# Own PSUM bank pairs for the norm products of the column stages, another split of the last convolution chunk, and a shifted row of gate chunks

## The chip, the cores and the metric

One core of a Trainium2 chip runs the whole network in one launch. The metric is the device time of the launch in microseconds (us). Engines are named as in the profile: PE (TensorE), PEld (its weight loads), DVE (VectorE), ACT (ScalarE), POOL (GpSimd) and SP (SyncE, which here only issues DMAs). Each engine works through its own queue in program order.

## The reference

The input x is 4 images of 256 channels, 56 by 56, in fp32. Four layers follow one another, each of the form x + f(groupnorm(x)), with 32 groups of 8 channels:

```python
x = x + _L0_conv_ref(_gn(x), ...)   # involution: 7x7 taps per pixel, from two 1x1 products
x = x + _L1_conv_ref(_gn(x), ...)   # relu(x + bn(conv3x3(relu(bn(conv3x3(x))))))
x = x + _L2_conv_ref(_gn(x), ...)   # involution with batch norms and relu
x = x + _L3_conv_ref(_gn(x), ...)   # x * (channel gate) + x * (spatial gate from DFTs)
```

A group norm needs the mean and variance of each channel, then an average over the 8 channels of a group, then rstd and shift.

## The kernel before

The two 128-channel halves of an image are "blocks"; a pair (image b, half cb) is a **unit**, so there are 8 units, u = 2b + cb. The kernel runs `involution_layer(0)`, then `conv_layer`, then `involution_layer(2)`, into which layer 3 is folded as "gates".

**An involution unit** has two stages. In the **tap stage** (`tap_matrices`), 32 steps n each make two PE products (L613) into a PSUM pair of banks, which DVE (two steps of three, L634) or ACT (one of three, L627) empties into `kt`. In the **column stage**, seven columns tx are taken in turn by `apply`: PE multiplies `kt` with the windows `xw` (L659), first for five plus five rows of tiles in one pair of banks, then for nine in a second pair; ACT (L672 or L674) and DVE (L679, three times and once) empty them; POOL (layer 0, L684) or DVE (layer 2, L686) adds the result to the image. After each column come a transposition of the next strip (L427, seven products, in a pair of its own), its copy by ACT (L439) and four DMAs that shift the windows (L445, L446, on SP's queue), the next strip (L410 or L412), and `column_sums` (DVE, L1143).

**PSUM** is a pool of four pairs (`two_banks`). A pair goes back when everything that was ever read from it or written to it is done, and the next one to need a pair takes it.

**Small work is hung between the big steps by hand.** `hooks[n]` runs after tap step n; `late[tx]` runs after column tx. A list item is one step of a generator. The order in which Python emits instructions is each engine's order (`in_order`). `norm_steps` (L217) is such a generator, with nine steps: aggregate (DVE, L215); product with the group-average matrix (PE, L226); copy, subtract, square, add (DVE, L229 to L237); second product (PE, L240); rsqrt (DVE L150, POOL L151); shift (DVE, L244). `by_counts(g, (1, 1, 4, 1, 1, 1))` makes six steps of these nine. In the column stages the two products go to `spare[0]`, which `apply` sets (L652) to the second, unused bank of its second pair:

```python
for ng, tys, nty, rows in O_PARTS:
    pair = two_banks()
    spare[0] = pair[:, 1, :]
```

Norms run this way in every unit of layer 0 but the last and in unit 0 of layer 2. In the tap stages `spare[0]` is a corner of the tap pair; `gate_factors`, `first_half` and the layer-3 norms use that. The last step of the last image's `gate_factors` is taken after the column stage of unit 7, where it uses whatever `spare[0]` is then.

**The bottleneck** of the next image (`bottleneck`, L454) makes `hb` from one small product (L467; L476 in layer 0, L478 in layer 2), the products L489, and 20 ACT evacuations (L506, or L508 in layer 2) into `hp`, which the next taps read.

**The convolution layer** works in 12 chunks of rows (three an image). In a chunk's `conv2` the positions k run in the order 1, 2, 3, 4, 0, 5; `filtered_product` makes four groups of products for a k in two pairs (L1606) and combines them on DVE (L1618 to L1624); `middle` is L1633 and L1634. `after[...]` lists are hung between these as above. At a chunk's end `joined(co)`, for each half co, forms the result and adds x. For chunk 10, `added` does it: ACT relu (L1764), an accumulating DMA from POOL (L1765), a store from SP (L1766). For chunk 11, the last, both halves are done on DVE (L1752, then L1757, which is relu and addition in one), with a store (L1758). Channel sums of chunks 9 to 11 are taken by DVE `bn_stats` (`stats`, L1784): those of chunk 10 inside chunk 11's `conv2`, those of chunk 11 (`pending[0]`, six instructions) all at hook 3 of layer 2's first tap stage. Earlier chunks use ACT instead (`mean_of`, `spread_of`, L1768 to L1778).

**The gates**: layer 2's finished images wait in DRAM. `gate_chunk` brings in a piece of 8 rows (POOL DMA, L828), works four POOL instructions on it (L831 to L838) and stores it (POOL DMA, L841); `next_load` and `next_gate` take one step each. An image has 14 chunks: four in the column stage of the next image's first half, six in the tap stage and four in the column stage of its second half.

Of the kernel before, what the change touches and what calls it, by code (L numbers as in the profile page):

```python
# [16 lines left out]
P = 128  # L17
# [56 lines left out]
def net_kernel(  # L74
# [243 lines left out]
    def involution_layer(layer, xin, xout, red, span, sb, xs_of, ahead=None, pending=None):  # L318

        with ExitStack() as es:  # L320
# [130 lines left out]
            def bottleneck(b):  # L451
# [23 lines left out]
                if layer == 0:  # L475
                    nc.vector.tensor_add(hb, ps[:, 0:1], by_row(L0_RB))  # L476
                else:
                    nc.vector.scalar_tensor_tensor(hb, ps[:, 0:1], bn["s3"], bn["t3"], ALU.mult, ALU.add)  # L478
# [167 lines left out]
            def apply(b, cb, kt, tx, xw):  # L646
# [3 lines left out]
                for ng, tys, nty, rows in O_PARTS:  # L650
                    pair = two_banks()
                    spare[0] = pair[:, 1, :]  # L652
# [337 lines left out]

            hooks0 = {}
            if layer == 0:
                place(hooks0, begin(), (1, 2, 4, 6, 7))
            else:
                since = mark()
                nc.sync.dma_start(z_sb, z2_dram)
                nc.sync.dma_start(zb_sb, zb2_dram)
                next_strip()
                run(bottleneck(0))
                hooks0[3] = list(pending[0])  # L1000
                for _ in range(NXW - 1):
                    next_windows()
                    next_strip()
                hooks0[7] = [next_windows, next_strip]
            if layer == 0:
                next_strip()
                for i in range(NXW):
                    hooks0.setdefault(2 + 5 * i, []).extend((next_windows, next_strip))
# [34 lines left out]
            for u, (b, cb) in enumerate(units):  # L1043
                hooks = hooks0 if u == 0 else {}
                if prev is not None:
# [39 lines left out]
                if b + 1 < B:  # L1085
                    if layer == 0:
                        g = sums(b + 1, cb)
                        if cb == 0:
# [3 lines left out]
                            def norm_first():  # L1092
                                yield from norm_of(0, {u + 2: sums_of[b + 1, 0]}, u + 2, u + 3)

                            g = norm_first()
                            for tx in (3, 4, 4, 4, 4, 4, 5, 5, 6):
                                late[tx].append(step(g))
                        else:
# [3 lines left out]
                            def norm_last():  # L1102
                                yield from norm_of(0, {u + 2: sums_of[b + 1, 1]}, u + 2, u + 3)
# [3 lines left out]
                            late[2] += [step(g)] * 5  # L1107
# [11 lines left out]
                if layer == 2 and b > 0:  # L1119
                    if cb == 0:  # L1120
                        late[0] += [lambda b=b, j=j: load_sf(b - 1, j) for j in range(2)]
                    for tx in (1, 2, 4, 5) if cb == 0 else (0, 2, 3, 5):
                        late[tx] += [next_load, next_gate]
                if last_image and cb == 0:
                    g = norm_of(1, {}, 0, u)
                    for tx in (1, 2, 2, 2, 2, 2, 3, 3, 4):
                        late[tx].append(step(g))
                if layer == 2 and u == 0:
                    g = norm_of(2, dict(enumerate(pending[1], NB * (B - 1))), NB * (B - 1), NB * B)
                    for tx in (1, 2, 2, 2, 2, 2, 3, 3, 4):  # L1130
# [90 lines left out]
    def conv_layer(xin, xout, st, ahead):  # L1221
        with ExitStack() as es:
# [474 lines left out]
            def conv2(i, after, between, sums, tail):  # L1697
# [28 lines left out]
                def joined(co):  # L1726
# [29 lines left out]
                    if i == n_chunks - 1:  # L1756
                        stt(xj, rj, 0.0, xj, ALU.max, ALU.add)  # L1757
                        nc.sync.dma_start(xout[bb][co][:, at], x)  # L1758
# [3 lines left out]
                def added(x, xj, rj, co, at):  # L1762
# [3 lines left out]
                    nc.sync.dma_start(xout[bb][co][:, at], x)  # L1766
# [13 lines left out]
                def stats(co, k):  # L1780

                    r0, r1 = k * ST_ROWS, min(n, (k + 1) * ST_ROWS)
                    at = sum(ST_PIECES[: i % 3]) + k
                    nc.vector.bn_stats(sums[co][:, at, :], xr_of[i, co][:, r0 * W : r1 * W])  # L1784
# [45 lines left out]
                if not summed or bb == B - 1:  # L1830
# [60 lines left out]
            for s, (conv, i) in enumerate(order):  # L1891
# [47 lines left out]
                else:  # L1939
                    if i % 3 == 0:  # L1940
# [3 lines left out]
                            else small.tile([P, sum(ST_PIECES), 6], F32, name=f"st_c{co}", bufs=1)  # L1944
# [151 lines left out]
```

## Time and profile before

| what | value |
|---|---|
| median of 3 runs | 1666.82 us (1665.92 to 1667.41) |
| profiled execution, its own time | 1665.74 us |
| its span, first to last instruction | 1663.7 us |
| mean granted TensorE clock | 0.979 |
| POOL, busy | 552.1 us (33%) |
| PEld, busy | 1442.0 us (87%) |
| layer 0 (first instruction to the last L659 before the convolutions) | 0 to about 502 us |
| convolutions (to the last L1606) | about 502 to 1119.4 us |
| first tap stage of layer 2 begins (L613) | 1141.47 us |
| last L659 of layer 2 ends, final phase begins | about 1631.5 us |

Times are from the start of the span. In a row of the timeline come the start, the time until the group ends, the engine, the line of the kernel, the operation, what is written and read with its shape, the count, and in brackets the idle time just before it with what ended it. In a row of the waits come the engine, what it wanted to run, what released it, and the total, the number and the longest of these waits. In a row of the windows come the stretch, its length, the busy time (and count) of PE, PEld, DVE, ACT and POOL, the granted clock, the share of the DMA engines' time and GB/s.

### The profile page before, as it was taken

Reading aid. Unit: us, or ns where it says so; the run is one execution under the profiler, and the core shown is the slowest. Engines: PE = TensorE matmul, PEld = TensorE weight load, DVE = VectorE, ACT = ScalarE, POOL = GpSimd, SP = SyncE. Lnnn points to the kernel's source line nnn. Section 1 sums busy time; section 2 is a strip of 40 time slices with the busy share of each in tenths; the row PEclk is TensorE's granted clock in tenths of the full one; section 3 lists DMA queues with packets and bytes.
Section 4 is the critical chain, followed back from the end, with each engine's and each line's share of the span. In section 5 each row is a group of like instructions: output and inputs, shape, how many; then the busy total and the mean of one; then the engine's idle time right before and its main releaser. Section 6 shows DMA issues by size and latency. Waiting matters only on the chain.

```text
span 1663.7 us, 57362 instructions
## 1 busy us (share of the span) xinstructions
PE 1586.3 (95%) x24600; PEld 1442.0 (87%) x24600; DVE 1328.1 (80%) x2391; ACT 1010.6 (61%) x2203; POOL 552.1 (33%) x764
## 2 busy tenths in 40 slices
PE   6999999999989999999999999988999899899998
PEld 4997998898888898899999999976888888788886
DVE  2686887787659988899999999987777678678775
ACT  1655655557446565666666567426677577577565
POOL 2133223322522343423333333200000662662671
PEclk9999999999999999999999999998999999999997
DMA  2363445444558977987788797744445765764753
GB/s 92 111 197 115 157 155 169 146 156 132 181 171 266 171 130 150 198 174 157 159 166 170 163 197 151 172 144 145 131 140 166 216 220 188 210 216 159 206 168 113
DMA packets 102875, 275.67 MB, mean 166 GB/s; under 512 B 15877, under 2 KB 43790, under 8 KB 98910
## 3 DMA queue, kind: packets, MB, share of 16 engines
q0 software_dynamic: 43856, 106.25, 31.3%
q1 hardware_dynamic: 57726, 164.48, 30.7%
q8 instruction: 195, 3.19, 0.8%
q10 hardware_dynamic: 1040, 1.26, 0.3%
q14 instruction: 58, 0.48, 0.1%
HBM read 95.07 MB, written 49.15 MB: 87 GB/s over the span
## 4 chain that ended last, share of the span: by engine, by line
PE 68%; DVE 13%; DMA 6%; issue 6%; ACT 4%; SPq 1%; POOL 1%; ACTq 0%; POOLq 0%; DVEq 0%
PE ps L613 21%; PE mm L1606 17%; PE ps L659 15%; PE mm L1591 6%; DVE un L679 3%; PE ps L427 3%; DMA xw<-xw 2%; DVE kt L634 2%; PE ps L489 2%; DMA xs<-x 1%; ACT hp L508 1%; DMA xs<-v 1%; SPq L445 1%; DVE st L380 1%; ACT xs L1737 1%
## 5 line engine op out<-in xcount | busy, mean ns | idle before, releaser
L659 PE MATMUL ps<-kt,xw 126*32 126x48 f32 (+1 forms) x12544 | 378.9, 235 | 23.1 <-DMA xw<-xw 9.6
L659 PEld LDWEIGHTS ps<-kt,xw 126*32 126x32 f32 (+1 forms) x12544 | 340.9, 121 | 66.3 <-issue 40.4
L613 PE MATMUL ps<-hp,z_sb 64*126 64x133 f32 x6144 | 376.0, 278 | 1.8 <-ACT hp L508 0.9
L613 PEld LDWEIGHTS ps<-hp,z_sb 64*126 64x126 f32 x6144 | 364.1, 186 | 13.1 <-DVE kt L634 6.0
L634 DVE TENSOR_TENSOR kt<-ps,zb_sb 126x798 f32<-126x798 f32 x352 | 331.9, 980 | 48.9 <-PE ps L613 29.8
L627 ACT ACTIVATE kt<-ps,zb_sb 126x133 f32<-126x133 f32 x960 | 280.5, 441 | 78.1 <-PE ps L613 78.1
L1606 PE MATMUL mm<-xs,u_sb 128*128 128x140 f32 (+2 forms) x1664 | 210.3, 279 | 4.2 <-DMA xs<-v 4.1
L1606 PEld LDWEIGHTS mm<-xs,u_sb 128*128 128x128 f32 x1664 | 200.8, 192 | 4.6 <-issue 4.5
L1591 PE MATMUL mm<-v,u_sb 128*128 128x280 f32 (+2 forms) x864 | 193.9, 383 | 2.4 <-DVE hp L1622 1.7
L1591 PEld LDWEIGHTS mm<-v,u_sb 128*128 128x128 f32 x864 | 161.6, 189 | 28.0 <-PE mm L1606 2.2
L684 POOL TENSOR_TENSOR xs<-un,xs 128x240 f32<-128x240 f32 x112 | 72.0, 663 | 298.8 <-DVE un L679 298.7
L679 DVE SCALAR_TENSOR_TENSOR un<-ps,s,un 128x240 f32<-128x240 f32 x224 | 102.5, 458 | 85.2 <-ACT un L674 79.2
L679 DVE SCALAR_TENSOR_TENSOR un<-ps,par_sb,un 128x240 f32<-128x240 f32 x224 | 97.7, 456 | 84.3 <-ACT un L672 80.2
L1574 POOL DMA_DIRECT2D xs<-v x100 | 96.6, 1003 | 182.8 <-ACT xs L1573 161.7
L672 ACT ACTIVATE un<-ps,par_sb 128x240 f32<-128x240 f32 x112 | 50.2, 448 | 131.8 <-PE ps L659 121.0
L439 ACT COPY xw<-ps 126x896 f32<-126x896 f32 x112 | 101.3, 905 | 39.8 <-PE ps L427 22.0
L427 PE MATMUL ps<-ident_sb,strip_sb 128*126 128x128 f32 x784 | 112.7, 285 | 5.2 <-POOL strip_sb L412 2.0
L674 ACT ACTIVATE un<-ps,bn_t,s 128x240 f32<-128x240 f32 x112 | 60.1, 538 | 92.3 <-PE ps L659 85.2
L427 PEld LDWEIGHTS ps<-ident_sb,strip_sb 128*126 128x126 f32 x784 | 85.8, 142 | 16.1 <-POOL strip_sb L412 3.7
L1606 PE MATMUL mm<-v_sb,u_sb 128*128 128x140 f32 (+2 forms) x688 | 95.2, 281 | 3.2 <-ACT u_sb L1353 1.8
L1606 PEld LDWEIGHTS mm<-v_sb,u_sb 128*128 128x128 f32 x688 | 88.4, 193 | 4.3 <-ACT u_sb L1353 2.0
L1573 ACT ACTIVATE xs<-v 128x560 f32<-128x560 f32 (+2 forms) x100 | 61.8, 629 | 44.3 <-DVE v L1518 35.9
(325 smaller groups left out, 2344.2 us busy)
## 6 DMA issues: line engine op xcount, KB each, us to landing
xw<-xw SPq DMA_DIRECT2D x224, 252.0 KB
xw<-xw SPq DMA_DIRECT2D x224, 126.0 KB
xs<-x POOLq DMA_DIRECT2D x24, 560.0 KB, 6.9
x<-xs POOLq DMA_DIRECT2D x8, 1568.0 KB, 8.1
xs<-x SPq DMA_DIRECT2D x8, 1568.0 KB
xs<-v POOLq DMA_DIRECT2D x44, 280.0 KB, 4.3
xs<-v POOLq DMA_DIRECT2D x42, 252.0 KB, 4.2
xs<-in_x_dram SPq DMA_DIRECT2D x6, 1568.0 KB
```

The lines of the kernel that those rows point to most:

```text
L427: nc.tensor.transpose(ps[:Q, k * P : (k + 1) * P], flat[:, k * Q : (k + 1) * Q], ident_sb)
L439: nc.scalar.copy(xw[:, :NSB, :], ps[:Q, : NSB * P].rearrange("q (n c) -> q n c", n=NSB))
L613: nc.tensor.matmul(ps[:Q, i, k * NT : (k + 1) * NT], z_sb[i * R : (i + 1) * R, cb * GB // 2 + gp, z0 : z0 + Q], hp[i * R : (i + 1) * R, py ...
L627: nc.scalar.activation(kt[:, g0 + i, pb, :, k], ps[:Q, i, k * NT : (k + 1) * NT], AF.Identity, bias=zb_sb[:, cb * GB + g0 + i, p0 + k : p0 ...
L634: nc.vector.tensor_tensor(kt[:, g0 : g0 + 2, pb], ps[:Q, :, : PB * NT].rearrange("q i (k t) -> q i t k", k=PB), zb_sb[:, cb * GB + g0 : cb ...
L659: nc.tensor.matmul(v[m * j : m * j + m, i, :, k * TP : (k + 1) * TP], xw[:, window(ty), m * j : m * j + m], kt[:, ng * j : ng * j + ng, :, ...
L679: nc.vector.scalar_tensor_tensor(part, o[e], s, part, ALU.mult, ALU.add)
L684: nc.gpsimd.tensor_tensor(dst, u, dst, ALU.add)
L1573: nc.scalar.mul(t[:, at], v[:, below], -1.0)
L1574: nc.gpsimd.dma_start(t[:, at], v[:, at], accum_op=ALU.add)
L1591: nc.tensor.matmul(ps, *position(u, v, ci, dy, k, co, n), start=(j == 0), stop=(j == NB * 3 - 1))
L1606: nc.tensor.matmul(ps[:, bank, co * m : (co + 1) * m], u[ci][:, co * P : (co + 1) * P], v2[:, : n // 2, ci * WT : (ci + 1) * WT], start=(c ...
```

## The change

Five edits are in one diff.

1. The norms of the column stages get `norm_between`: the two products go each to a pair of their own (`one_bank`), in the six steps of `by_counts`, and the steps are spread anew over the columns. For image b + 1's first half in layer 0 the products stand after columns 4 and 6, the four DVE steps after column 5, and the shift moves to hook 5 of the next unit; for its second half both stand where they did; for the two norms of units 6 (layer 0) and 0 (layer 2) the six steps stand after columns 1 to 6. `apply` no longer sets `spare[0]`.
2. In layer 2, `hb` is made by ACT instead of DVE.
3. Chunk 11, half 0, ends like chunk 10 (ACT relu, accumulating DMA from POOL); half 1 stays on DVE. The two stores become entries of `pending[0]`.
4. Chunk 10's sums are taken by ACT (`mean_of`, `spread_of`, twice each), after the last `filtered_product`'s first part; the layout of the sums changes to triples. `pending[0]`, now two stores and six `bn_stats`, is spread over hooks 3, 5, ..., 17 of layer 2's first tap stage.
5. The gates of images 0 and 1 are spread three, six, four and one over four stages: three after columns 1, 3, 5, and one at hook 1 of the stage after next. Image 2 keeps four, six and four.

```diff
-                    nc.vector.scalar_tensor_tensor(hb, ps[:, 0:1], bn["s3"], bn["t3"], ALU.mult, ALU.add)
+                    nc.scalar.activation(hb, ps[:, 0:1], AF.Identity, bias=bn["t3"], scale=bn["s3"])
...
                     pair = two_banks()
-                    spare[0] = pair[:, 1, :]
...
+            def norm_between(layer, sts, u0, u1):
+                return by_counts(norm_steps(sts, one_bank, layer, u0, u1), (1, 1, 4, 1, 1, 1))
...
-                hooks0[3] = list(pending[0])
...
+                for n, f in enumerate(pending[0]):
+                    hooks0.setdefault(3 + 2 * n, []).append(f)
...
+                if layer == 2 and cb == 0 and b > 1:
+                    hooks[1].insert(0, next_gate)
...
+                if layer == 0 and cb == 1 and b + 1 < B:
+                    place(hooks, first, (5,))
...
-                            g = norm_first()
-                            for tx in (3, 4, 4, 4, 4, 4, 5, 5, 6):
+                            g = first = norm_first()
+                            for tx in (3, 4, 5, 6, 6):
                                 late[tx].append(step(g))
...
                             late[1].append(step(g))
-                            late[2] += [step(g)] * 5
+                            late[2] += [step(g)] * 2
                             late[3] += [step(g)] * 3
...
-                    for tx in (1, 2, 4, 5) if cb == 0 else (0, 2, 3, 5):
+                    for tx in (0, 2, 3, 5) if cb else (1, 2, 4, 5) if b == B - 1 else (1, 3, 5):
                         late[tx] += [next_load, next_gate]
...
-                    g = norm_of(1, {}, 0, u)
-                    for tx in (1, 2, 2, 2, 2, 2, 3, 3, 4):
+                    g = norm_between(1, {}, 0, u)
+                    for tx in range(1, 7):
...
-                    if i == n_chunks - 1:
+                    if i == n_chunks - 1 and co == 1:
                         stt(xj, rj, 0.0, xj, ALU.max, ALU.add)
-                        nc.sync.dma_start(xout[bb][co][:, at], x)
+                        tail.append([lambda: nc.sync.dma_start(xout[bb][co][:, at], x)])
                     else:
                         added(x, xj, rj, co, at)
...
-                    nc.sync.dma_start(xout[bb][co][:, at], x)
+                    store = lambda: nc.sync.dma_start(xout[bb][co][:, at], x)
+                    if i < n_chunks - 1:
+                        store()
+                    else:
+                        tail.append([store])
...
-                if not summed or bb == B - 1:
+                if i == n_chunks - 2:
+                    for f in (mean_of, spread_of):
+                        tail.append([lambda co=co, f=f: f(sums[co][:, 2 * ST_PIECES[0]], xr_of[i, co][:, : n * W]) for co in range(NB)])
+                elif bb == B - 1:
                     tail += [[lambda co=co, k=k: stats(co, k) for k in range(ST_PIECES[i % 3])] for co in range(NB)]
...
-                    loads_at = (2, 4) if i < n_chunks - 1 else (4, 7)
-                    for at, fs in zip(loads_at, tail2):
+                    for at, fs in zip((2, 4), tail2):
                         for k, f in enumerate(fs):
-                            after[at - (k == 0)].append(f)
+                            after[at - (k == 0) if i < n_chunks - 1 else 10].append(f)
```

More of the change, by code (lines that the diff above doesn't have):

```diff
@@ L1092, in norm_first @@
                             def norm_first():
-                                yield from norm_of(0, {u + 2: sums_of[b + 1, 0]}, u + 2, u + 3)
-                            g = norm_first()
-                            for tx in (3, 4, 4, 4, 4, 4, 5, 5, 6):
+                                yield from norm_between(0, {u + 2: sums_of[b + 1, 0]}, u + 2, u + 3)
+                            g = first = norm_first()
+                            for tx in (3, 4, 5, 6, 6):
                                 late[tx].append(step(g))
@@ L1102, in norm_last @@
                             def norm_last():
-                                yield from norm_of(0, {u + 2: sums_of[b + 1, 1]}, u + 2, u + 3)
+                                yield from norm_between(0, {u + 2: sums_of[b + 1, 1]}, u + 2, u + 3)
                             g = norm_last()
                             late[1].append(step(g))
-                            late[2] += [step(g)] * 5
+                            late[2] += [step(g)] * 2
                             late[3] += [step(g)] * 3
@@ L1121, in involution_layer @@
                         late[0] += [lambda b=b, j=j: load_sf(b - 1, j) for j in range(2)]
-                    for tx in (1, 2, 4, 5) if cb == 0 else (0, 2, 3, 5):
+                    for tx in (0, 2, 3, 5) if cb else (1, 2, 4, 5) if b == B - 1 else (1, 3, 5):
                         late[tx] += [next_load, next_gate]
                 if last_image and cb == 0:
-                    g = norm_of(1, {}, 0, u)
-                    for tx in (1, 2, 2, 2, 2, 2, 3, 3, 4):
+                    g = norm_between(1, {}, 0, u)
+                    for tx in range(1, 7):
                         late[tx].append(step(g))
                 if layer == 2 and u == 0:
-                    g = norm_of(2, dict(enumerate(pending[1], NB * (B - 1))), NB * (B - 1), NB * B)
-                    for tx in (1, 2, 2, 2, 2, 2, 3, 3, 4):
+                    g = norm_between(2, dict(enumerate(pending[1], NB * (B - 1))), NB * (B - 1), NB * B)
+                    for tx in range(1, 7):
                         late[tx].append(step(g))
@@ L1782, in stats @@
                     r0, r1 = k * ST_ROWS, min(n, (k + 1) * ST_ROWS)
-                    at = sum(ST_PIECES[: i % 3]) + k
-                    nc.vector.bn_stats(sums[co][:, at, :], xr_of[i, co][:, r0 * W : r1 * W])
+                    at = 2 * k + (2 * ST_PIECES[0] + 1) * (i == n_chunks - 1)
+                    st = sums[co][:, at : at + 2, :].rearrange("p a b -> p (a b)")
+                    nc.vector.bn_stats(st, xr_of[i, co][:, r0 * W : r1 * W])
                 for n_s, k in enumerate(KS[:5]):
@@ L1943, in conv_layer @@
                             if i // 3 < B - 1
-                            else small.tile([P, sum(ST_PIECES), 6], F32, name=f"st_c{co}", bufs=1)
+                            else small.tile([P, 2 * (ST_PIECES[0] + ST_PIECES[2]) + 1, 3], F32, name=f"st_c{co}", bufs=1)
                             for co in range(NB)
```

## The prediction

> **What bounds the kernel.** I read the busy shares of the page, then PE's waits, then the timeline at the places that the diff touches.
>
> ```profile
> PE 1586.3 (95%) x24600; PEld 1442.0 (87%) x24600; DVE 1328.1 (80%) x2391; ACT 1010.6 (61%) x2203; POOL 552.1 (33%) x764
> ```
>
> PE is busy nearly throughout, so a gain must come out of its idle time, place by place. The waits say where:
>
> ```profile
> ACT hp L508 <- DVE hb L478: 22.3, 1, 22.3
> ...
> PE ps L659 <- DMA xw<-xw: 9.6, 8, 3.6
> ...
> PE ps L467 <- DVE hp L1624: 5.2, 1, 5.2
> ...
> PE ps L226 <- DVE un L679: 4.9, 7, 1.0
> ...
> PE ps L240 <- DVE un L679: 4.4, 8, 1.0
> ...
> DVE st_c L1784 <- DMA u_sb<-x: 3.4, 1, 3.4
> ```
>
> Lines 4 and 5 are the norm products (9.3 us in 15 waits); lines 1, 3 and 6 belong to one place, the passage from the convolutions to layer 2; line 2 is where gate traffic could matter.
>
> **1. Norm products, -7.7 us.** A norm column of layer 0:
>
> ```profile
> 207.83 1.82 DVE L679 SCALAR_TENSOR_TENSOR un<-ps,par_sb,un 128x240 f32<-128x240 f32 x4 [0.72 <-ACT un L672]
> ...
> 208.22 0.98 PE L427 MATMUL ps<-ident_sb,strip_sb 128*126 128x128 f32 x7
> ...
> 209.56 0.62 DVE L1143 BATCH_NORM_STATS2 st<-xs 128x6 f32<-128x448 f32 x1
> ...
> 209.70 0.38 PE L226 MATMUL ps<-mv_sb,gavg_sb 128*128 128x1 f32 x2 [0.50 <-DVE un L679]
> ...
> 210.12 0.16 DVE L229 COPY gm<-ps 128x1 f32<-128x1 f32 x1
> ```
>
> PE is done with the transposition at 209.20, but the product writes a bank of the pair that DVE's fourth L679 still empties until 209.65, and waits 0.50. Its own input (L215) had been ready since 207.1. In a pair of its own it starts at once: all 9.3 us go. The Trainium skill (PSUM — Partial Sum Buffer, Summary: rules for kernel authors) says one may read PSUM while a matmul runs if the bank differs, and to guard by bank; by that rule alone the product could have run in its bank all along, part 1 would give nothing and the sum would be 1658. The row shows the program waiting nevertheless, so the row decides.
>
> What comes back: a fifth user of four pairs. The next `apply` then needs the pair of the `apply` just before, free when its third L679 is done. In layer 2 that is 1186.89 (row at 1185.41, 1.48 long), with the transposition over at 1186.76: 0.13 late, which the product itself (0.3) covers. Where the copy stands one column later, the pair is held for that column, and the following `apply` has no product to cover it: some 0.2 each. That is 7 times (three first halves, two products each in units 6 and 0): 1.4, and 0.2 for the rest. The nearest row is L467, a product already in its own pair at the same spot: the `apply` behind it started without a wait at 1235.20, but after 0.54 at 1359.66 and, in the same place one image on, 0.78. So the ends are -9.3 (nothing back) and +3.2 (0.78 after each of 16). I take -9.3 + 1.6, by the two rows of the columns themselves.
>
> **2. The passage into layer 2, -8.8 us.** DVE, then ACT and PE:
>
> ```profile
> 1109.92 0.63 DVE L1784 BATCH_NORM_STATS2 st_c<-u_sb 128x6 f32<-128x448 f32 x1 [3.43 <-DMA u_sb<-x]
> ...
> 1124.52 1.39 DVE L1752 SCALAR_TENSOR_TENSOR u_sb<-hp,s,u_sb 128x1120 f32<-128x1120 f32 x1
> 1125.94 2.20 DVE L1757 SCALAR_TENSOR_TENSOR xs<-u_sb,xs 128x1120 f32<-128x1120 f32 x1
> ...
> 1129.46 2.27 DVE L1757 SCALAR_TENSOR_TENSOR xs<-u_sb,xs 128x1120 f32<-128x1120 f32 x1
> ```
>
> ```profile
> 1133.29 8.34 ACT L508 ACTIVATE hp<-ps,hb,bn_s 64x168 f32<-64x168 f32 x20 [22.27 <-DVE hb L478]
> ```
>
> ```profile
> 1141.47 7.82 PE L613 MATMUL ps<-hp,z_sb 64*126 64x133 f32 x96 [0.85 <-ACT hp L508]
> ```
>
> The path is DVE to 1131.7, memsets, `hb` at 1133.07, ACT's 20 evacuations, taps. Six `bn_stats` of chunk 10 leave DVE (2.7 us), and with them the 3.43 wait for x. DVE takes L1618 at 1106.5, not 1110.46. Position 4 then waits for ACT's copy (L1617, over at 1108.7) and for PE (done 1110.2): 1110.95. L1810 to L1813 take 2.7 (1113.7), position 0 with `middle` 3.6 (1117.3), position 5 2.4 (1119.7). So L1752 stands at 1119.7, 4.8 earlier; L467 follows PSUM's release, so PE's 5.16 wait shrinks to under 2. One L1757 of two goes: L1752 twice (1122.5), L1757 once, DVE done at 1124.6, 7.1 earlier.
>
> ACT gets what DVE loses: `mean_of` 1.12 + 0.19 + 0.20 and `spread_of` 0.19 + 1.23 + 0.19 per half (rows L1771 to L1778), 6.2 in all, then a relu of 2.28 (row L1764). The means write x in place, so they wait for chunk 10's stores (L1766, issued from 1109.95). Those are over by 1116:
>
> ```profile
> 1116.00:1128.00 12.00, 6.84 (x39) 4.86 (x39) 11.65 (x17) 0.00 (x0) 0.00 (x0) 0.74 0.00 1
> ```
>
> (busy times of PE, PEld, DVE, ACT, POOL; then clock, DMA share, GB/s). ACT is idle in all of it, and no DMA runs. The first mean fits before 1116, the rest ends by 1120.7, before the relu can begin (1121.1). Relu to 1123.4, `hb` on ACT 0.2, and the evacuations start at 1123.7, not 1133.29: 9.6 earlier.
>
> Behind DVE and ACT stands all that allocates from the freed convolution memory: POOL's strip memset and strip (0.83 + 0.89, ready 1126.5, no later than PE), and SP's loads. SP loses two stores ahead of them (3.9 us of its time); `z_sb`, issued at 1133.5 before and used at 1141.47, is issued at 1126.4 and here by 1134.4 at the latest. POOL's accumulating DMA runs beside it. Taps so begin between 1131.9 and 1134.4; I take 1132.7, -8.8. PE's clock is the open end:
>
> ```profile
> 1140.00:1146.00 6.00, 5.15 (x47) 4.78 (x48) 2.49 (x4) 4.30 (x9) 0.00 (x0) 0.53 0.23 75
> ```
>
> The first 48 tap products ran at 0.53 and took 5.03 (chain of waits), against 2.9 at the 60 ns of the next 276: 2.1 to gain if that is spared. Products, two transpositions and then taps follow one another as thinly after the change, so I take 0. (The Trainium skill, TensorE: Matmul & The Clock Gate, HAM oscillation, wants no PE gap over some 3.4 us; by it the 5.16 gap, once under 2, would leave the clock up, 2.1 us better.) Ends: -11.7, and -4.8 (only DVE's own head start, ACT 4 us late).
>
> **3. Last `bn_stats`, -0.5.** All six stood at hook 3: 2.70 us on the chain at 1147.52, PE idle 0.40 and 0.48 around. Spread over 11 steps they need 2.7 of DVE's slack (two L634 of 0.91 in 2.05 us leave 0.9 in 12 steps, the transposition 1.0); the rest is eaten by the pairs ahead, or not. Ends -0.9 and +0.8.
>
> **4. Gates, -0.4.** POOL is not held by columns:
>
> ```profile
> 1326.75 0.54 POOL L841 DMA_DIRECT2D out_dram<-gx  x1
> 1335.97 0.56 POOL L151 TENSOR_TENSOR norm_sb<-norm_sb,mhalf 128x1 f32<-128x1 f32 x1 [8.68 <-DVE norm_sb L150]
> ```
>
> It takes six gates back to back from 1293.8 and is stopped only by the norm's power at step 12 of the next taps. With three instead of four in the column stage, five run before that stop, at the same pace: PE's 3.63 wait for `xw` at 1303.11 falls in the second gate and stays. Only the sixth (1321.8 to 1327) leaves the end of the stage, where waits of 0.4 stand. The fourteenth runs after 1382, beside taps. Ends -3.6 (that wait goes) and +0.6.
>
> **5. `hb` on ACT, three more times, 0**: 0.2 moves from DVE to ACT while PE works elsewhere; the waits behind L467 are for L679. Ends -0.6 and +0.6. **Unit 7, +0.9**: `spare[0]` is now the last tap pair, kept until the gate factors' product at the very end; the column stage has three pairs. Each `apply` behind a transposition (four) waits the 0.13 to 0.25 of part 1. Ends 0 and +4.7 (0.78 six times).
>
> **Sum.** -7.7 - 8.8 - 0.5 - 0.4 + 0 + 0.9 = -16.5. The profiled execution took 1665.74 (span 1663.7, 2.0 around it): 1649.2. The median of the runs is 1.1 higher: 1650.
>
> **Rivals.**
> - *The new pairs are the new wait.* If a held pair makes PE wait until DVE's copy, some 1.1 after the transposition (209.20 to 210.28), 7 times: 7.7 comes back in place of 1.6, 1656. For: DVE trails PE in every column. Against: another pair is free earlier.
> - *ACT or z_sb is late*, part 2 gives -4.8: 1654.
> - *The gates do relieve the windows*, -3.6: 1647. Against: POOL's pace.
> - *Slower: ACT's queue.* Four sums and a relu stand ahead of `hb` and the 20 evacuations. If the stores that the means wait for land late, each us moves the taps by one. Parts 1, 3, 4 and 5 give -7.7, so no change if the evacuations start at 1133.3 + 7.7 = 1141, and 0.2% slower from 1144.3: 1671 at 1145. It needs stores 20 us later than the 0.00 DMA share above allows.
> - *The diff does little*: 1666.
>
> **Chances.** Forecast (1646 to 1653) 0.57; pairs 0.15; ACT or z_sb 0.13; gates 0.09; slower 0.04; little 0.02. A measurement tells about 0.2% (3.3 us) from no change. Faster 0.94, within 0.2% 0.02, slower 0.04. The range reaches from the gates' case with the clock spared (1644) over the pairs' case (1658).
>
> **What would show it.** L226 and L240 without a wait on L679; under 0.3 before the `apply` behind. No L1784 between L1808 and L1618; L1752 near 1119.7 less what layer 0 saved; L508 starting some 9.6 earlier relative to the last L1606 of chunk 10; five gates before L151. Wrong if L659 waits on L229's copy, if L1771 ends after 1121, or if L613 waits for z_sb.

## The result and the profile after

| what | before | after |
|---|---|---|
| median | 1666.37 us (4 runs, 1664.09 to 1667.41) | 1645.28 us (4 runs, 1639.19 to 1647.76) |
| ratio, 95% interval | | 0.987, 0.9839 to 0.9901 |
| profiled execution, its own time | 1665.74 | 1639.19, the fastest of its four |
| span | 1663.7 | 1636.8 |
| mean granted clock | 0.979 | 0.985 |
| last L1606 (after: L1614) of chunk 11 to first tap product of layer 2 | 22.09 | 14.32 |

The changed kernel is 21 us faster; the forecast was 1650, in a range of 1644 to 1658. The median lies in the range and 0.7 us below the band of 1646 to 1653 that had the chance of 0.57. One of the six runs of the last experiment, 1666.73, was in a slow state and is left out of its ratio. Behind line 651 most line numbers moved: `apply`'s products are L658 (L659 before), its DVE step L678 (L679), the chunks' products L1599 and L1614 (L1591, L1606). The profiled execution is 6 us faster than its median, so what stands in one trace is read at the places of the change only, and a second profile of the changed kernel is used beside it (last experiment).

From the page of after, and from its waits (engine, line, released by: total, number, longest):

```profile
PE 1575.3 (96%) x24600; PEld 1435.7 (88%) x24600; DVE 1326.7 (81%) x2380; ACT 1020.6 (62%) x2220; POOL 555.5 (34%) x767
```

```profile
PE ps L658 <- DMA xw<-xw: 12.2, 15, 2.6
...
PE ps L658 <- DVE un L678: 5.8, 15, 1.2
...
PE ps L467 <- DVE hp L1632: 2.0, 1, 2.0
```

The waits of L226 and L240 for DVE's `un` and that of `st_c` are gone, and L467's is down from 5.2 to 2.0. L658's for DVE is up from 2.5 (5 times) to 5.8 (15 times): 1.2 of it stood there before, behind L489; 1.4 is three waits right behind L226, 1.4 is six waits a column later, and 1.7 is in unit 7. Those three parts came back, and with them some 0.13 at each of twelve places right behind the products (1.5 in all), too short for this row. The waits for windows are no smaller (9.6 before).

A norm column of layer 0 in the timeline of after, the one shown in the prediction:

```profile
204.09 1.82 DVE L678 SCALAR_TENSOR_TENSOR un<-ps,par_sb,un 128x240 f32<-128x240 f32 x4 [0.72 <-ACT un L671]
204.47 0.98 PE L427 MATMUL ps<-ident_sb,strip_sb 128*126 128x128 f32 x7
...
205.29 0.28 PE L226 MATMUL ps<-mv_sb,gavg_sb 128*128 128x1 f32 x2
...
205.71 3.27 PE L658 MATMUL ps<-kt,xw 126*64 126x96 f32 x112
...
208.91 0.98 PE L427 MATMUL ps<-ident_sb,strip_sb 128*126 128x128 f32 x7
...
210.11 3.26 PE L658 MATMUL ps<-kt,xw 126*64 126x96 f32 x112 [0.22 <-DVE un L678]
...
210.76 0.14 DVE L229 COPY gm<-ps 128x1 f32<-128x1 f32 x1
```

The product follows the transposition at once, while DVE still works (to 205.91) on the pair that it used to wait for, and the `apply` behind it starts 0.13 later. One column on, the product's pair is still held (its copy, L229, comes at 210.76), and the `apply` there waits 0.22 for L678. The passage into layer 2, same view:

```profile
1108.29 0.60 PE L467 MATMUL ps<-norm_sb,red_sb 128*128 128x1 f32 x4 [2.02 <-DVE hp L1632]
...
1108.93 0.35 ACT L478 ACTIVATE hb<-ps,bn_t,bn_s 128x1 f32<-128x1 f32 x1 [1.35 <-PE ps L467]
...
1109.69 2.26 ACT L1772 ACTIVATE xs<-u_sb 128x1120 f32<-128x1120 f32 x1 [0.40 <-DVE u_sb L1760]
...
1112.39 8.36 ACT L508 ACTIVATE hp<-ps,hb,bn_s 64x168 f32<-64x168 f32 x20 [0.43 <-PE ps L489]
...
1120.59 3.65 PE L613 MATMUL ps<-hp,z_sb 64*126 64x133 f32 x59 [0.91 <-DVE hp L497]
```

The last L1614 ended at 1106.27. ACT's evacuations start 6.1 behind it (13.9 before), the taps 14.3 behind it. What holds them in this trace is PE's own L489, whose first eight products took 3.42. In four other traces with the same passage (m_changed, e_spare, f_at3, k_gates0) the taps waited for z_sb, 1.1 to 2.0.

### The profile page after: what moved, and what is told of

Same layout as the page of the kernel before. It is cut to its first block, busy times and chain, and to the rows that moved or that the text cites. A ratio compares the mean times of both kernels' runs of the same rounds, so it can differ in the third digit from the quotient of the medians.

```text
span 1636.8 us, 57403 instructions
## 1 busy us (share of the span) xinstructions
PE 1575.3 (96%) x24600; PEld 1435.7 (88%) x24600; DVE 1326.7 (81%) x2380; ACT 1020.6 (62%) x2220; POOL 555.5 (34%) x767
## 4 chain that ended last, share of the span: by engine, by line
PE 73%; DVE 9%; DMA 6%; ACT 4%; issue 3%; SPq 2%; POOL 2%; ACTq 0%; POOLq 0%; DVEq 0%
PE ps L613 21%; PE mm L1614 20%; PE ps L658 14%; PE mm L1599 9%; DMA xw<-xw 4%; PE ps L427 3%; DVE un L678 2%; DVE kt L634 2%; PE ps L489 2%; SPq L445 1%; ACT hp L508 1%; SPq L446 1%; DMA xs<-v 1%; DMA xs<-x 1%; PE ps L971 1%
## 5 line engine op out<-in xcount | busy, mean ns | idle before, releaser
L658 PE MATMUL ps<-kt,xw 126*32 126x48 f32 (+1 forms) x12544 | 376.5, 234 | 25.6 <-DMA xw<-xw 12.2
L658 PEld LDWEIGHTS ps<-kt,xw 126*32 126x32 f32 (+1 forms) x12544 | 338.9, 121 | 70.1 <-issue 44.1
L613 PE MATMUL ps<-hp,z_sb 64*126 64x133 f32 x6144 | 374.1, 277 | 2.7 <-DVE hp L497 0.9
L613 PEld LDWEIGHTS ps<-hp,z_sb 64*126 64x126 f32 x6144 | 361.8, 185 | 13.5 <-DVE kt L634 6.1
L1614 PE MATMUL mm<-xs,u_sb 128*128 128x140 f32 (+2 forms) x1664 | 208.8, 278 | 1.8 <-DMA xs<-v 1.8
L1614 PEld LDWEIGHTS mm<-xs,u_sb 128*128 128x128 f32 x1664 | 199.7, 191 | 2.1 <-issue 1.7
L1599 PE MATMUL mm<-v,u_sb 128*128 128x280 f32 (+2 forms) x864 | 193.7, 382 | 1.5 <-DVE hp L1630 1.5
L1599 PEld LDWEIGHTS mm<-v,u_sb 128*128 128x128 f32 x864 | 161.8, 189 | 26.9 <-PE mm L1614 1.8
L678 DVE SCALAR_TENSOR_TENSOR un<-ps,s,un 128x240 f32<-128x240 f32 x224 | 102.5, 457 | 79.7 <-ACT un L673 75.5
L678 DVE SCALAR_TENSOR_TENSOR un<-ps,par_sb,un 128x240 f32<-128x240 f32 x224 | 97.9, 456 | 75.9 <-ACT un L671 71.9
L439 ACT COPY xw<-ps 126x896 f32<-126x896 f32 x112 | 101.4, 906 | 39.5 <-PE ps L427 21.9
L427 PEld LDWEIGHTS ps<-ident_sb,strip_sb 128*126 128x126 f32 x784 | 83.6, 140 | 14.7 <-POOL strip_sb L412 4.5
L1614 PE MATMUL mm<-v_sb,u_sb 128*128 128x140 f32 (+2 forms) x688 | 94.3, 279 | 2.1 <-ACT u_sb L1361 2.1
L1614 PEld LDWEIGHTS mm<-v_sb,u_sb 128*128 128x128 f32 x688 | 87.3, 191 | 3.0 <-ACT u_sb L1361 2.3
```

Source lines behind the costliest of these rows:

```text
L427: nc.tensor.transpose(ps[:Q, k * P : (k + 1) * P], flat[:, k * Q : (k + 1) * Q], ident_sb)
L439: nc.scalar.copy(xw[:, :NSB, :], ps[:Q, : NSB * P].rearrange("q (n c) -> q n c", n=NSB))
L613: nc.tensor.matmul(ps[:Q, i, k * NT : (k + 1) * NT], z_sb[i * R : (i + 1) * R, cb * GB // 2 + gp, z0 : z0 + Q], hp[i * R : (i + 1) * R, py ...
L658: nc.tensor.matmul(v[m * j : m * j + m, i, :, k * TP : (k + 1) * TP], xw[:, window(ty), m * j : m * j + m], kt[:, ng * j : ng * j + ng, :, ...
L678: nc.vector.scalar_tensor_tensor(part, o[e], s, part, ALU.mult, ALU.add)
L1599: nc.tensor.matmul(ps, *position(u, v, ci, dy, k, co, n), start=(j == 0), stop=(j == NB * 3 - 1))
```

## The experiments

Times are medians beside runs of the kernel before on the same chip, whose own medians were 1661.9 to 1666.4. "Passage" is the time from the last product of chunk 11 to the first tap product of layer 2; "to the norm" that from there to unit 0's first L226, less the wait before that L226; "window waits" are PE's idle times between two products of `apply` in a unit's column stage. These three are read from each kernel's one trace. Five traces (after, m_changed, e_spare, f_at3, k_gates0) have the changed kernel's passage and differ elsewhere: theirs is 14.17 to 15.11, so one trace tells a passage to about half a us. A ratio and its interval can differ by up to 0.2% from the quotient of the two medians beside them.

**1. The norm products alone (a_norms).** Edit 1 without the removed line of `apply`.

```diff
-                    g = norm_of(1, {}, 0, u)
+                    g = norm_between(1, {}, 0, u)
...
```

> The kernel before with edit 1 alone (pairs of their own for the norm products of the column stages; apply still sets spare[0], so unit 7 is as before). My theory, part 1: the 15 waits of L226 and L240 for L679 (9.3 us) go and 1.6 come back, so 7.7 less than before, about 1658.7 beside 1666.4; in its trace no product waits for L679, and the apply behind a product starts at most 0.5 late, only where the copy stands a column later. Rival (the new pairs are the new wait): PE waits about 1.1 at seven places until DVE's copy, so only 1.6 less. Rival (by the rule that only a shared bank has to be guarded): nothing changes, within 1 us of before.

Measured: 1656.87 beside 1665.55, ratio 0.9939 (0.9912 to 0.9966). No L226 or L240 waits for L679 (9.33 us in the trace of before). Right behind them stand 2.66 in all: 0.47 to 0.48 at three, 0.10 to 0.14 at ten. Six more waits of 0.24 to 0.28 (1.5 in all) stand at the `apply` one column later, where the pair is still held. So 5.2 is the gain at these places, half a us under the interval of the times (5.7 to 14.7 us). The theory holds but for the size of what comes back. Both rivals fall: 1.6 or nothing lie outside the interval.

**2. The passage alone (b_passage).** Edits 3 and 4, `hb` on DVE.

```diff
-                    if i == n_chunks - 1:
+                    if i == n_chunks - 1 and co == 1:
...
+                if i == n_chunks - 2:
+                    for f in (mean_of, spread_of):
...
```

> The kernel before with edits 3 and 4 alone (end of the convolutions; hb stays on DVE). My theory, parts 2 and 3: 8.8 and 0.5 less, no more, so 9.3 less than before, about 1657; PE's gap before L467 falls from 5.2 to 2. Second theory, from the trace of the whole change, where the first taps run at full clock and PE's 1.34 gap inside chunk 11 is gone: 1.3 and 2.1 more, so 12 to 13 less, about 1654. Rival (ACT or the tables late): 4.8 less, about 1661.6, with L613 waiting for z_sb or L508 for the second sum.

Measured: 1654.88, ratio 0.9939 (0.9915 to 0.9963), so 6 to 14 us less, which tells neither theory from the other. By the trace the passage is 16.59 (5.5 less) and the 1.34 inside chunk 11 is gone; PE's wait for L467 is 2.02. The rival is not seen: its 4.8 lies outside the interval, L613 waits for L508 and L508 for `hb`. The 1.34 comes and goes with x, though: in the four traces with chunk 10's sums on DVE, the wait of `st_c` for x is 1.9, 2.5, 3.1 and 3.4, and PE's wait inside chunk 11 is 0, 0.44, 1.0 and 1.34 (a_norms, h_sums10, c_gates, before). The clock was not spared: 0.61 over the first 4 us of taps. So the second theory's 2.1 did not come in this trace, and the passage is 2.3 longer than in the changed kernel, because ACT waited 2.73 for `hb`.

**3. The gates alone (c_gates).** Edit 5.

```diff
+                if layer == 2 and cb == 0 and b > 1:
+                    hooks[1].insert(0, next_gate)
...
-                    for tx in (1, 2, 4, 5) if cb == 0 else (0, 2, 3, 5):
+                    for tx in (0, 2, 3, 5) if cb else (1, 2, 4, 5) if b == B - 1 else (1, 3, 5):
```

> The kernel before with edit 5 alone (gate chunks three, six, four and one). My theory, part 4: POOL runs the gates at its own pace, so the 3.63 wait for xw in unit 2 stays: 0.4 less, which can't be told from no change. Rival (the gates relieve the windows): 3.6 less, about 1662.8, with that wait gone or halved.

Measured: 1666.95, ratio 1.0005 (0.9981 to 1.003). Window waits of units 2 and 4: 4.8 and 2.5 (before 4.2 and 5.7). POOL stored five gates ahead of L151 instead of six, as the prediction had it. The rival's 3.6 is outside the interval, by little.

**4. `spare[0]` back in `apply` (e_spare).**

```diff
                     pair = two_banks()
+                    spare[0] = pair[:, 1, :]
```

> The changed kernel with one line back: apply sets spare[0] to the unused bank of its second pair, so that unit 7's column stage has four pairs again. My theory (unit 7): 0.9 less than the changed kernel, so 22 less than before where the changed kernel is 21 less. Rival (three pairs are a wait in every column): up to 4.7 less than the changed kernel. Rival (they cost nothing): the same as the changed kernel.

Measured: 1650.2, ratio 0.9897 (0.9864 to 0.993), too wide for 0.9. By the traces: in unit 7 the changed kernel waits 0.28 and 0.26 for L678 behind two transpositions (in both of its profiles; 0.26 to 0.27 behind a third in three other traces), this one nowhere. It also waits 1.18 at the second column, which follows the first without a transposition between. After, then this kernel:

```profile
1579.99 3.23 PE L658 MATMUL ps<-kt,xw 126*64 126x96 f32 x112 [1.18 <-DVE un L678]
```

```profile
1584.59 6.90 PE L659 MATMUL ps<-kt,xw 126*64 126x96 f32 x224
```

The 1.18 stands in all seven traces with three pairs in unit 7 and in none of the seven with four. So three pairs cost 1.7 to 2.0 in waits there, not 0.9, and no wait in every column. The stage's length does not tell it (29.6 to 32.2 with four pairs, 30.0 to 33.5 with three), for its waits for windows vary by more.

**5. `hb` back on DVE (d_hb_dve).**

```diff
-                    nc.scalar.activation(hb, ps[:, 0:1], AF.Identity, bias=bn["t3"], scale=bn["s3"])
+                    nc.vector.scalar_tensor_tensor(hb, ps[:, 0:1], bn["s3"], bn["t3"], ALU.mult, ALU.add)
```

> The changed kernel with edit 2 undone (hb of layer 2 on DVE again). My prediction put edit 2 at nothing in the units and counted hb on ACT inside the passage. Theory now, from edits 3 and 4 alone, where hb stood on DVE behind the second L1758 and the strip's memset and L508 began 8.4 after the last convolution product (6.1 in the changed kernel): L508 begins about 2.3 later than in the changed kernel, taps about 2 later, units alike, so some 2 slower than the changed kernel. Rival (ACT's relu or the tables hold the passage anyway): the passage is as long as in the changed kernel, 14.3.

Measured: 1651.31, ratio 0.9898 (0.9867 to 0.9929). The passage is 17.32, 3.0 longer than in after (2.2 to 3.2 against the five traces); the rival is out. Timeline:

```profile
1118.67 0.20 DVE L404 MEMSET strip_sb<- 128x168 f32 x1 [1.81 <-POOL strip_sb L391]
1118.78 0.10 DVE L478 SCALAR_TENSOR_TENSOR hb<-ps,bn_s,bn_t 128x1 f32<-128x1 f32 x1
...
1118.99 8.34 ACT L508 ACTIVATE hp<-ps,hb,bn_s 64x168 f32<-64x168 f32 x20 [2.47 <-DVE hb L478]
```

On DVE the one-column `hb` stands behind L1765 and a memset that waits for POOL; ACT waits 2.47 for it.

**6. Half 0 back on DVE (g_half0).**

```diff
-                    if i == n_chunks - 1 and co == 1:
+                    if i == n_chunks - 1:
```

> The changed kernel with edit 3 undone (both halves of chunk 11 end on DVE; no relu on ACT, no accumulating DMA at the end). My theory, part 2: one L1752 and L1757 stand between the last convolution and the freed memory, one L1757 (2.3) more than in the changed kernel, so everything that allocates from it (strip, z_sb) is 2.3 later; L508 itself, with hb on ACT and no relu ahead, starts no later. Taps 1 to 2.3 later. Rival (the accumulating DMA and z_sb collide, so that edit 3 costs what it saves): taps no later than in the changed kernel, z_sb landing in less time from its issue.

Measured: 1644.68, ratio 0.9873 (0.9824 to 0.9922). Passage 15.21, 0.9 longer than in after, and 0.1 to 1.0 against the five traces. z_sb is issued 2.2 later, as the theory said, but the taps do not wait for it. They wait for ACT, which starts late for a reason that neither theory had:

```profile
1110.19 1.39 DVE L1760 SCALAR_TENSOR_TENSOR u_sb<-hp,s,u_sb 128x1120 f32<-128x1120 f32 x1
...
1111.70 8.36 ACT L508 ACTIVATE hp<-ps,hb,bn_s 64x168 f32<-64x168 f32 x20 [3.72 <-DVE u_sb L1760]
```

L508 writes `hp`, and the wait ends with the second L1760, the last reader of the convolutions' `hp`. With edit 3 both L1760 stand back to back; without it an L1765 of 2.2 stands between them. L489's first eight products, which ACT needs too, began at 1107.52 and at after's 3.42 were done by some 1110.9, so the extra wait is only the last 0.7. The rival (a collision that eats the gain) is not shown: the taps don't wait for z_sb. Edit 3 is worth up to 1.0, not 2.3, and the times don't tell it.

**7. Chunk 10's sums back on DVE (h_sums10).**

```diff
-                if i == n_chunks - 2:
-                    for f in (mean_of, spread_of):
-                        tail.append([lambda co=co, f=f: f(sums[co][:, 2 * ST_PIECES[0]], xr_of[i, co][:, : n * W]) for co in range(NB)])
-                elif bb == B - 1:
+                if bb == B - 1:
...
+                    loads_at = (2, 4) if i < n_chunks - 1 else (4, 7)
...
```

> The changed kernel with chunk 10's sums back on DVE (six bn_stats inside chunk 11's second convolution). My theory, part 2: DVE loses 4.8 there (the wait for x, then 2.7 of work), PE waits about 1.3 inside chunk 11 and about 5 instead of 2 before L467, so the taps come 4 to 5 later: 4 to 5 slower than the changed kernel. Rival (the sums were hidden; the gain came from edit 3 and hb alone): at most 1 later.

Measured: 1651.75, ratio 0.9929 (0.9901 to 0.9956): 12 less than before, where the changed kernel was 21 and, in its second set, 19 less. Passage 18.20, 3.9 longer than in after (3.1 to 4.0 against the five); inside chunk 11 PE waits 0.44. From its waits:

```profile
PE ps L467 <- DVE hp L1632: 5.2, 1, 5.2
...
DVE st_c L1797 <- DMA u_sb<-x: 2.5, 1, 2.5
```

Both waits of before are back. So of the passage's 7.8, by leaving out one at a time, chunk 10's sums are 3.9, `hb` 3.0 and half 0 0.9, each to about half a us.

**8. All of `pending[0]` at hook 3 (f_at3).**

```diff
-                for n, f in enumerate(pending[0]):
-                    hooks0.setdefault(3 + 2 * n, []).append(f)
+                hooks0[3] = list(pending[0])
```

> The changed kernel with all of pending[0] (two stores, six bn_stats) at hook 3 of layer 2's first tap stage. My theory, part 3: PE idles twice, 0.4 and 0.5, around the run of six, and waits nowhere else for them: the first taps' stage 0.5 to 0.9 longer than in the changed kernel. Rival: spread or not, DVE has the slack, and the stage is within 0.2.

Measured: one run, 1652.3. Around the six (2.78 on DVE) PE waits 0.42 and 0.47, as before; the changed kernel has one wait of 0.64 in its taps instead, for ACT's `kt` (so have all the kernels with the hooks spread). Spreading is worth 0.25: between the two theories.

**9. No gate in the first column stage (k_gates0).** Images 0 and 1: none, seven, four and three.

```diff
-                    hooks[1].insert(0, next_gate)
+                    for n, f in ((1, next_load), (1, next_gate), (3, next_load), (3, next_gate), (5, next_gate)):
+                        hooks.setdefault(n, []).append(f)
...
-                        for n in (2, 6, 14, 18, 22, 26):
+                        for n in (2, 6, 14, 18, 22, 26) if b == B - 1 else (2, 6, 10, 14, 18, 22, 26):
...
-                    for tx in (0, 2, 3, 5) if cb else (1, 2, 4, 5) if b == B - 1 else (1, 3, 5):
+                    for tx in (0, 2, 3, 5) if cb else (1, 2, 4, 5) if b == B - 1 else ():
```

> The changed kernel with the gates of images 0 and 1 spread none, seven, four and three (hooks 1, 3 and 5 of the stage after next) over the four stages, instead of three, six, four and one; image 2 as it was. In the eight kernels so far the column stages of units 2 and 4 hold 5 to 11 us of PE's waits for windows xw, those of units 1 and 3 at most 3, whether three or four gates are issued there. Theory (part 4: POOL runs five gates there in either kernel, and their transfers hold up the windows): with none issued, the waits of units 2 and 4 fall from some 8 together to under 2, and none appear in the tap stages: 6 to 7 less than the changed kernel, 27 less than before. Rival (the windows are late of themselves): units 2 and 4 keep 5 or more, no gain. Rival (the waits move): units 3 and 5 gain what 2 and 4 lose.

Measured: 1647.19 beside 1661.91, ratio 0.9916 (0.9894 to 0.9939): not better than the changed kernel by its ratio. Window waits of units 2 and 4: 2.0 and 2.0, between the theory's under 2 together and the rival's 5. They did not go; POOL still stored three gates there (five in the changed kernel), but that these hold up the windows is not shown. Units 3 and 5 hold 1.1 and 0.0, so nothing moved.

**10. Three small edits (j_mends).**

```diff
-                return by_counts(norm_steps(sts, one_bank, layer, u0, u1), (1, 1, 4, 1, 1, 1))
+                return by_counts(norm_steps(sts, one_bank, layer, u0, u1), (1, 2, 3, 1, 1, 1))
...
                     pair = two_banks()
+                    spare[0] = pair[:, 1, :]
...
             if layer == 2:
+                nc.sync.dma_start(z_sb, z2_dram)
+                nc.sync.dma_start(zb_sb, zb2_dram)
                 sin_sb = wpool.tile([H, H], F32, name="sin_sb")
...
```

> The changed kernel with three small edits at three places: norm_between in steps of 1, 2, 3, 1, 1, 1, so that the copy of the first product stands in the product's own column; spare[0] set in apply again; z_sb and zb_sb ahead of the two tables in SP's queue. Theory (the held pair costs the three waits of 0.48 behind L226; unit 7's transpositions are followed by 0.25 only with three pairs; z_sb is what L613 waits for where the clock stays up through L489): the 0.48 become 0.1 to 0.15, unit 7's 0.28 and 0.26 go, and L613 does not wait for z_sb: 1.5 to 2.4 less than the changed kernel, at the edge of what the times can tell. Rival on the copy (DVE now waits for PE's product with its column's work queued behind): the 0.48 stay or appear one apply later.

Measured: 1650.04, ratio 0.9934 (0.9908 to 0.9959): no gain over the changed kernel by the times. The three 0.48 stay (0.47, 0.47, 0.48). My theory of them falls, and so does the rival's reason: in those units the copy stood in the product's column already. Timeline of after at one of them:

```profile
136.53 0.34 DVE L215 BATCH_NORM_AGGREGATE mv_sb<-st 128x2 f32<-128x42 f32 x1
...
136.79 1.75 DVE L678 SCALAR_TENSOR_TENSOR un<-ps,par_sb,un 128x240 f32<-128x240 f32 x4
...
137.59 0.28 PE L226 MATMUL ps<-mv_sb,gavg_sb 128*128 128x1 f32 x2
...
138.34 3.27 PE L658 MATMUL ps<-kt,xw 126*64 126x96 f32 x112 [0.48 <-DVE un L678]
```

The wait is for L678, the release of the `apply` before, and L678 begins late because L215 and three sums of the next image (L380, 1.66) stand ahead of it on DVE. Where the pair really is held for a column, the `apply` right behind the product waits at most 0.14; the price comes one column later, 0.22 to 0.27 at six places in after (1.40 in all). Here the copy of the first product stands in the product's own column, and four of the six are gone. Timeline of j_mends at the place shown for after:

```profile
209.72 0.14 DVE L229 COPY gm<-ps 128x1 f32<-128x1 f32 x1
...
213.17 3.31 PE L659 MATMUL ps<-kt,xw 126*64 126x96 f32 x112
```

The two that stay (0.22 and 0.26) belong to the second products of unit 6 and of layer 2's unit 0, whose pair this edit still holds for a column. Unit 7's waits for L678 are gone. z_sb is issued 7.16 behind the last convolution product (7.99 in after), and L613 waits for DVE's copy; the passage is 14.39.

**11. Both (l_all).** Experiments 9 and 10 in one kernel.

```diff
+                    for n, f in ((1, next_load), (1, next_gate), (3, next_load), (3, next_gate), (5, next_gate)):
...
+                return by_counts(norm_steps(sts, one_bank, layer, u0, u1), (1, 2, 3, 1, 1, 1))
...
```

> Both at once: the gates none, seven, four and three, and the three small edits. Theory: the sum, 8 to 9 less than the changed kernel, some 29 less than before. Rival (windows late of themselves): only the small edits, 2 less than the changed kernel.

Measured: 1640.44 (1635.57 to 1641.88), ratio 0.9879 (0.9856 to 0.9902); passage 13.94, window waits of units 2 and 4 2.7 and 2.8. All five runs are below the six of j_mends on the same chip (1644.2 to 1655.97), which has the gates of the change. That points to the gates as a gain here; but k_gates0 against the changed kernel shows none, and the twelve other traces hold 5.2 to 10.5 in these two units, this one 5.5. Whether it beats the changed kernel stays open.

**12. The changed kernel again (m_changed).** No edit.

> The changed kernel once more, for more runs and a second profile of it. Edits 1, 3 and 4, and 5 alone measured -0.61%, -0.61% and +0.05%, together 1.17% or 19.5 us; edit 2 is worth 2 to 3 us inside the passage by its traces. Theory (the parts add up): 1.1 to 1.4% less than before, the passage 14 to 15 long, the waits for windows of units 2 and 4 5 or more together, and slower by 5 to 9 us than the kernel with the gates spread none, seven, four and three and the three small edits, where the chip is the same. Rival (the first four runs of the changed kernel were lucky): under 1% less.

Measured: 1648.74 (6 runs, 1640.31 to 1666.73) beside 1664.85, ratio 0.9884 (0.9846 to 0.9922). The parts add up within the intervals: 0.61, 0.61 and -0.05% make 1.17%, the whole 1.3 and 1.2%. The rival's "under 1%" lies inside this interval too, so these runs do not rule it out. The chip was another than that of l_all, so the two are not compared. Its profiled execution, 1656.84, has the same places: 2.8 right behind the norm products and 1.2 a column later, passage 14.82. Timeline:

```profile
1115.58 2.24 ACT L1772 ACTIVATE xs<-u_sb 128x1120 f32<-128x1120 f32 x1
...
1117.91 8.35 ACT L508 ACTIVATE hp<-ps,hb,bn_s 64x168 f32<-64x168 f32 x20
...
1126.77 5.80 PE L613 MATMUL ps<-hp,z_sb 64*126 64x133 f32 x96 [1.42 <-DMA z_sb<-z_dram]
```

Here x came late (ACT's first sum waited 3.99 for it), the four sums ended 3.5 behind the last convolution product (1.3 in after), and L508 started right behind the relu, no later than in the first profile (6.0 behind the last product). The taps then waited for z_sb.

## Why the prediction was right, step by step

| step | predicted | measured at its place |
|---|---|---|
| 1, norm products | -9.3 + 1.6 | -9.3 + 4.3 (after), + 4.0 (second profile) |
| 2, passage | -8.8 | -7.8 and -7.3, with the 1.34 inside chunk 11 of before: -9.1 and -8.6 |
| 2, clock at the taps | 0, with 2.1 open | to the norm 39.80 before, 37.56 after; 2.0 without the `bn_stats`' share |
| 3, `bn_stats` | -0.5 | -0.25 |
| 4, gates | -0.4 | no change that can be told |
| 5, `hb` in the units | 0 | not told apart |
| unit 7 | +0.9 | +1.7 |
| sum | -16.5 | -5.0 - 9.1 - 2.0 - 0.25 + 1.7 = -14.6 |

The measured terms make 1651.8 of the median before. They are a little short of the first ratio's interval (16.5 to 26.8 us less) and inside that of the second set (13.0 to 25.6). The trace of after is 26.9 shorter; most of what goes beyond 15 lies where the diff changes nothing: the start of the kernel (first taps at 43.62 instead of 45.69) and the convolutions ahead of chunk 11 (5.5 shorter; L1606's waits for transfers fall from 4.1 to 1.8). So the mechanisms were right. That the sums lie so near is luck in part: the terms that were off have both signs, and the clock's 2.0 did not come in every trace of this passage.

*Step 1.* The product's wait went as said. The held pair came back as said too: 0.2 at seven places, 1.4 in all, was forecast; after has 0.22 to 0.27 at six, 1.40 in all, and experiments 10 and 11 take away the four of them that they should. What the prediction missed is the place right behind the product, where it had 0.2 in all and after has 2.9: some 0.13 at twelve places, which the product was to cover and did not, and three waits of 0.48, over the 0.3 that the prediction gave as its sign, which are DVE's late L678, behind sums in its own queue. The rival (1.1 at each held pair) is refuted by experiments 1 and 10.

*Step 2.* The head start of DVE by chunk 10's sums (4.8 said) is 4.3 by experiment 7: 3.9 in the passage and PE's 0.44 inside chunk 11. The second L1757 (2.3 said) is worth 0.9 by experiment 6, since L508 needs the last L1760, not the last L1765, and z_sb was not late without edit 3. `hb` is worth 3.0: on DVE it would have followed L1765 and the memsets. Part 5 names only its 0.2, but the sum had about 2.5 for it without saying so, as the difference between DVE's 7.1 and the evacuations' 9.6. Each of these is good to about half a us, as the five traces show. "ACT or z_sb late" came in the second profile, with 1.42 at L613 instead of the 4 us of the rival, and in three more traces of that passage. That is one of the signs by which I said I would be wrong, and the step held all the same; in those four traces it is z_sb's landing that ends the passage. The rival of ACT's queue was not seen: in m_changed the sums ended by 1115.4, just after the relu could have begun, which was another such sign, and the evacuations were not later.

*Clock.* I took 0 of 2.1, and both profiles of the changed kernel have the 2.1. The reason that the prediction left open, L467's gap under 2, is not what did it: in both profiles the clock fell to 0.50 behind that gap of 2.0 and was up again at the taps. Of the five traces of this passage, e_spare and f_at3 did not have the 2.1 (38.8 and 39.5 to the norm), so it is a matter of the run, as the last section shows.

*Step 4.* Five gates before L151, and nothing gained, as said; the rival that they relieve the windows by 3.6 is out by experiment 3, by little.

*Unit 7.* The four small waits were forecast as 0.9 and are 0.54 (0.8 in three other traces); the 1.18 at the column that follows without a transposition was not seen, so the term is mis-sized by 0.8.

## What to carry to other kernels

Where a small step waits for an engine, look at everything in that engine's queue ahead of it: the one-column `hb` was worth some three us because a long step and a wait for freed memory stood before it on DVE and nothing on ACT. A wait that goes gives back what the next resource lacks, so look at which release comes next and at the queue of the engine that makes it. A buffer that is held longer is paid for where the next user is short of one, here one column after the product. When the waits for transfers vary by several us from run to run, times settle only large parts; small ones are settled by the same place in several traces.

## What the runs showed of the hardware

**The clock after a short gap depends on more than the gap.** Ten traces have the same wait of 2.0 before L467. In eight of them the granted clock then fell to 0.50 for some 3 us; in e_spare and f_at3 it stayed at 1.00. Windows of after, from the end of the convolutions (length, busy times of PE, PEld, DVE, ACT, POOL, clock, DMA share, GB/s):

```profile
1106.27:1109.27 3.00, 0.98 (x7) 0.72 (x8) 2.83 (x5) 1.65 (x3) 0.00 (x0) 0.96 0.00 0
1109.27:1112.27 3.00, 3.00 (x10) 0.93 (x8) 2.96 (x3) 2.28 (x2) 0.02 (x1) 0.50 0.00 0
...
1120.59:1124.59 4.00, 4.00 (x70) 4.00 (x72) 2.84 (x4) 4.00 (x10) 0.00 (x0) 1.00 0.22 67
```

and of e_spare, where it held there and fell at the taps:

```profile
1113.24:1117.24 4.00, 3.98 (x22) 1.74 (x24) 3.96 (x3) 3.22 (x6) 0.00 (x0) 1.00 0.00 0
...
1121.24:1126.12 4.88, 1.85 (x8) 1.38 (x8) 2.10 (x4) 4.80 (x12) 1.00 (x1) 0.62 0.75 233
1126.12:1130.12 4.00, 4.00 (x43) 4.00 (x45) 1.92 (x2) 1.63 (x3) 0.00 (x0) 0.61 0.47 140
```

In e_spare L489 ends 1.7 sooner, which brings nothing, because L613 then waits 1.81 for z_sb; and its first 4 us of taps hold 43 products instead of 70. Over all fourteen traces the first 4 us of taps had the clock at 1.00 in six (to the norm 37.3 to 37.6) and at 0.50 to 0.61 in eight (38.8 to 40.5). The gaps just before the taps don't sort them: k_gates0 waited 1.97 there and kept 1.00, f_at3 1.09 and had 0.50. The Trainium skill (TensorE: Matmul & The Clock Gate, HAM oscillation) asks only for gaps under some 3.4 us; here a wait of 2.0 and four products of one column were followed by the lower clock in eight traces of ten, and the measurement decides. The same page (What's actually happening) calls the window over which activity is judged free-running, so that a change of the clock depends on where in it the work falls.

The traces agree with that, and show the window: in each of the fourteen, all changes of the granted clock lie on one grid of 3.41 us. The steps of that grid around the wait, in after and then in e_spare:

```profile
1105.62:1109.03 3.41, 1.39 (x12) 1.16 (x12) 3.23 (x6) 2.03 (x6) 0.00 (x0) 1.00 0.00 0
1109.03:1112.44 3.41, 3.41 (x10) 0.98 (x8) 3.38 (x3) 2.57 (x3) 0.19 (x1) 0.50 0.00 0
1112.44:1115.85 3.41, 3.41 (x17) 0.97 (x13) 2.28 (x5) 3.36 (x9) 2.70 (x7) 1.00 0.61 81
```

```profile
1108.75:1112.16 3.41, 2.49 (x21) 2.28 (x20) 3.29 (x6) 2.93 (x7) 0.00 (x0) 1.00 0.01 2
1112.16:1115.57 3.41, 2.31 (x14) 1.18 (x16) 3.27 (x4) 2.60 (x5) 0.00 (x0) 1.00 0.00 0
...
1118.99:1122.40 3.41, 1.71 (x13) 1.27 (x11) 2.69 (x5) 3.33 (x9) 2.30 (x7) 1.00 0.94 160
1122.40:1125.81 3.41, 1.75 (x7) 1.35 (x7) 1.21 (x3) 3.36 (x9) 0.10 (x1) 0.50 0.71 261
```

In after the whole wait falls into one step, PE is busy for 1.39 of its 3.41, and the next step has 0.50. In e_spare a step ends inside the wait, so that each of two steps holds a part of it, with PE busy for 2.49 and 2.31, and the clock stays; it falls ahead of the taps, behind a step with 1.71. The wait before L467 lies alike in all ten: a step ends 2.2 to 3.3 behind the last convolution product in the eight traces where the clock fell, and 0.9 and 1.1 behind it, inside the wait, in the two where it held. No run moved the grid on purpose, so this is read from ten traces and not tested; how busy PE must be in a step is not shown.

**The memory of a dead tile is a wait of its own.** In g_half0 what ended ACT's wait of 3.72 was DVE's last read of the convolutions' `hp`, some 0.7 after its own input was there by the estimate of experiment 6. That is one trace, and the releaser is the one that its profile names.
